# Output projection of a retention block by seven products of halves, with the work around it moved, on one Trainium2 core

## The chip, the cores and the metric

The kernel runs on one core of one Trainium2 chip. The metric is the device time of one execution in microseconds, lower is better. A core has five engines that run beside each other and wait for each other by semaphores: TensorE (PE in the profile; its weight loads are PEld), VectorE (DVE), ScalarE (ACT), GpSimd (POOL) and SyncE (SP), which here issues nearly all transfers.

## The reference

One attention-like layer and one feed-forward layer, each behind a layer norm and each inside a residual sum. x has 4 x 1024 tokens of 512 features.

```
# x: (4, 1024, 512)
h   = layernorm(x)
q   = h @ Wq.T                      # 512 x 512
v   = h @ Wv.T
ret = scan(v): state = lam * state + v_t    # along the tokens, lam by head
o   = layernorm(q * ret) * gamma + beta
o   = (o * silu(h @ Wg.T)) @ Wo.T
x   = x + layernorm(o)
h   = layernorm(x)
g   = silu((h @ fp8(gate_w)) * gate_scale)  # 512 -> 1536
u   = (h @ fp8(up_w)) * up_scale
x   = x + layernorm(((g * u) @ fp8(down_w)) * down_scale)
```

Here `fp8(w)` means that the weights are rounded to 8-bit values and used as float32 again.

## The kernel before

The 4096 tokens are cut into 8 blocks of 512 (`TB`), a block into 4 tiles of 128 tokens. A block t goes through `Retention` (the attention layer up to the normalised and turned x1) and then through `Ffn`. The main loop (L985 to L1205 or so) interleaves three of them: in its pass t it runs the feed-forward layer of block t (`f`), the retention of block t+1 (`b`), and the loading and normalising of x of block t+2 (`n`); `l` is the feed-forward layer of block t-1, whose last rows and final norm are finished in the first passes. Each pass t has 12 rows i (`NI`): in a row TensorE does the gate group (`f.gate(i)`, L1027), the up group (`f.up(i)`, L1088) and the down group two rows behind (`f.down(i - f.lag)`, L1155), eight matmuls each, and between them whatever the retention of the next block has due. "Block 1" in what follows means the pass t = 1 of this loop, "row" its i.

The order of the work on every engine is the order of the program text: `InOrder` (L66) wraps each engine, so that every instruction has line L74 in the profile and groups must be read by their tiles: `pfg`, `pfu`, `pd` are gate, up and down of the feed-forward layer, `pv`, `pq`, `pg` and `po` the four projections of the retention, `pt` a turn (transposition) by TensorE, `t_sums` the input sums, `mids` the partial results, `seen` the output of the search (below).

PSUM: the retention uses two banks, `pa0` and `pa1`, one buffer each; the gate and up groups use a ring of two (`pf`), into which the turns with home `"pf"` are taken as well; the down groups have four.

From block 2's retention on (`FAST`, so in passes t = 1 to 6) the v, q and g projections are not done as 16 full matmuls but in Strassen's manner by seven products of half size (`product`, L466). Each product is four matmuls of 128 x 256; its weight half (or a stored sum of halves) comes from a ring of four buffers `w_ring`, which `fetch_weights` (L369) refills over SP, one fetch behind each product. The right-hand sides are the halves of the turned x, or one of four differences `t_sums` that POOL makes (`input_sums`, L450). Products share two banks: some matmuls add onto a bank whose earlier content VectorE or ScalarE has to have read first. The order of the 21 products and their banks stand in `order` and `banks` (L332 to L336). The products are called at fixed places: behind the gate group (L1035), behind the up group (L1100), at the end of a row (L1169, L1176, L1180).

The output projection (`o`, L657) is direct in every block: rows 7 to 10 each do one tile of 128 tokens by four matmuls of 128 x 512 in full float32 from the weights in `wo_sb`. Behind each tile stand, on the tile's own result in PSUM: moments (`o_moments`, L665, VectorE and POOL), centring (`x1_of`, L668; `center_scale` on VectorE in these blocks), the residual addition (POOL) and its store (`kept`), moments of the sum (`x1_moments`), its normalising (`x1n_of`, VectorE), and the turn: tiles 0 to 2 by a VectorE transposition in small squares and a way through memory (`move_x1n` and `turn_by_blocks`, L311: four stores, one load), the last one by TensorE (`turn_x1n`). Both halves of the turned tile, the rounded upper and the remainder (`upper_of` on ScalarE, `rest_of` on VectorE), go into `x1nT`, which the next block's first gate group reads.

The x of the block after next is normalised on ScalarE (`norm_x`), transposed in squares on VectorE, stored (`send_x`) in rows 6 to 9, and fetched back turned (`fetch_x`) at the end of row 9. From block 3's x on, `norm_x` uses one buffer of tag `xn`, so each tile waits for the store of the one before.

In pass t = 1 ScalarE also searches all weights for values out of range in 24 steps (`find_over`, L223); the list `look` (L983) says how many of them each row takes, half of them behind the gate group and the rest later in the row (L1032, L1126).

Of the kernel before, what the change touches and what calls it, by code (L numbers as in the profile page):

```python
# [23 lines left out]
def retention_ffn_sandwich(  # L24
# [20 lines left out]
    NT, D = x.shape  # L45
# [177 lines left out]
    def find_over():  # L223


        k = 0
        for j in range(4):
            for w in (gate_sb, up_sb, down_sb):
                v = w[:, ts(j, NI // 4), :] if w is down_sb else w[:, :, ts(j, I // 4)]
                for sign in (1.0, -1.0):  # L230
                    tag = "ret" if k >= 16 else "xn"
                    seen = work.tile(list(v.shape), F8, tag=tag, name=f"seen_{k}", bufs=2 if k >= 16 else 1)
                    act.activation(
                        seen, v.bitcast(F32), AF.Relu, bias=neg_max, scale=sign,
                        accum_out=over[:, k : k + 1], saturate=False,
                    )
                    k += 1
                    yield
# [72 lines left out]
    def turn_by_blocks(dst, src, tag, name):  # L311


        t = work.tile([P, NQ, NC, Q], F32, tag=tag, name=name)
        dve.transpose(t, src.rearrange("p (c a i) -> p a c i", c=NC, a=NQ))
        m = dram.tile([P, NQ, NC, Q], F32, tag="turn", name=f"m{name}", bufs=2)
        for b in range(NQ):
            sp.dma_start(
                m[:, b].rearrange("(a i) c j -> i a (c j)", a=NQ),
                t[ts(b, Q)].rearrange("i a c j -> i a (c j)"),  # L320
            )
        sp.dma_start(dst, m)

# [12 lines left out]
    banks = {"v": {1: 0, 6: 1, 5: 0}, "q": {1: 1, 6: 0, 5: 1}, "g": {1: 0, 6: 0, 5: 1}}  # L336
    squares = {"v": (wvT, wv_sb), "q": (wqT, wq_sb)}
    operands = {}

# [16 lines left out]

    made = {}
    adding = weight_sums()

    def keep_sums(k):  # L360
        for j, t in made[k].items():
            operands[k][j] = dram.tile([P, 2, H], F32, tag=f"sum_{k}{j}", name=f"dsum_{k}{j}", bufs=1)
            sp.dma_start(operands[k][j], t)
# [5 lines left out]
    def fetch_weights():  # L369
        n = fetched[0]  # L370
        if n < total_products:
            k, j = order[n % len(order)]
            sp.dma_start(w_ring[:, n % RING], operands[k][j])
            fetched[0] += 1

    class Retention:
# [89 lines left out]
        def product(self):  # L466

            k, j = order[self.made]
            n = (self.t - FAST) * len(order) + self.made
            self.made += 1  # L470
            w = w_ring[:, n % RING]
            if j in (1, 6, 5):
                bank = ps_tile(f"p{k}{j}_{self.t}", f"pa{banks[k][j]}").rearrange("p (c f) -> p c f", c=2)
                if j == 6:
                    self.bank_b = bank
                else:
                    self.bank_a = bank
            bank = self.bank_b if j in (6, 7, 4) else self.bank_a
            for o in range(2):
                out_ = bank[:, o]  # L480
                if len(self.right[j].shape) == 4:
                    out_ = out_.rearrange("p (g j) -> p g j", j=Q)
                for c in range(2):
                    pe.matmul(
                        out_, w[:, c, ts(o, P)], self.right[j][:, c],
                        start=(j in (1, 6, 5) and o == 0 and c == 0), stop=True,
                        skip_group_check=True,
                    )
            fetch_weights()
            c12, p1, s167 = (mids[:, m] for m in (1, 2, 3))  # L490
            if j == 1:
                act.copy(p1, bank)
            elif j == 6:
                dve.tensor_tensor(c12, bank, p1, ALU.add)
            elif j == 7:
                dve.tensor_tensor(s167, bank, p1, ALU.add)
            elif j == 2:
                self.take(k, 0, 0, bank)
            elif j == 4:
                dve.tensor_tensor(p1, bank, p1, ALU.add)  # L500
                self.take(k, 1, 0, p1)
            elif j == 5:
                dve.tensor_tensor(s167, bank, s167, ALU.add)
                self.take(k, 1, 1, s167)
            else:
                dve.tensor_tensor(c12, bank, c12, ALU.add)
                self.take(k, 0, 1, c12)

        def take(self, k, o, h, src):

# [156 lines left out]

        def x1_of(self, s):  # L668
            self.x1n[s] = work.tile([P, D], F32, tag="tok", name=f"x1n_{self.t}_{s}", bufs=4)
            self.center(self.x1n[s], self.po.pop(s), self.mvo[s])  # L670
            pool.tensor_tensor(self.xt[s], self.xt[s], self.x1n[s], ALU.add)
            self.kept[s] = dram.tile([P, D], F32, tag="kept", name=f"kept_{self.t}_{s}")
            sp.dma_start(self.kept[s], self.xt[s])
# [18 lines left out]
        def move_x1n(self, s):  # L692

            x1n = self.x1n.pop(s)
            dst = x1n.rearrange("p (b c j) -> p b c j", b=NQ, c=NC)
            turn_by_blocks(dst, x1n, "ret", f"xs1_{self.t}_{s}")
            self.pt[s] = dst.rearrange("p b c j -> p c b j")

        def part(self, h, s):
            part = self.x1nT[:, h, :, ts(s, P)]  # L700
# [279 lines left out]

    look = [5, 5, 4, 2, 0, 0, 0, 2, 2, 2, 2, 0]  # L983
    l = None
    for t in range(NB):  # L985
        f, n = Ffn(a), None
        fast = b is not None and b.fast
        for i in range(NI):
# [28 lines left out]
                n.shift()  # L1017
            if b and not fast and i == 5:
                b.z(0)
            if b and i >= 8:  # L1020
                b.x1_moments(i - 8)
            if t == 0 and 8 <= i < 11:
                for _ in range(4):
# [49 lines left out]
            if b and 7 <= i <= 10:  # L1073
                b.o(i - 7)
            if b and i == 8:
                b.new_x1nT()
            if b and i >= 8:
                b.x1n_of(i - 8)
            if b and 8 <= i < 11:
                b.move_x1n(i - 8)  # L1080
            if b and i >= 9:
                b.upper_of(i - 9)
            if b and 7 <= i <= 10:
# [44 lines left out]
            if l and not b and i in (4, 5):  # L1128
# [3 lines left out]
                    l.rstd()  # L1132
            if n and i == 6:
                n.new_xnT()
            if b and 7 <= i <= 10:
                b.x1_of(i - 7)
            if b and i >= 9:
# [7 lines left out]
            if n and i == (9 if t else 7):  # L1145
                n.fetch_x()
            if b and n and i == 11 and t:
                b.rest_of(3)
            if t == 0 and i in (8, 9):
                keep_sums("vq"[i - 8])  # L1150

# [4 lines left out]
            elif l and i < 2 and (b or i == 0):  # L1156
                l.down(NI - 2 + i if b else NI - 1)
            if b and not n and i == 11:
                b.turn_x1n(3)
# [107 lines left out]
```

## Time and profile before

| | |
|---|---|
| Median of 3 runs | 984.25 us (983.97 to 984.66) |
| The profiled execution | 983.95 us, span 982.1 us |
| TensorE clock granted | 0.998 of full |
| `po` matmuls | 256 records, 114.5 us |
| `pv`, `pq`, `pg` matmuls by halves (all six blocks) | 1008 records, 238.4 us |
| DMA | 110.07 MB, mean 112 GB/s, 36.5% of the 16 engines |
| VectorE, longest groups | `fuse` remainders 74.5 us, `gate` products 71.7 us |

A full float32 matmul leaves two records in the trace. The profile gives, for each group of instructions, its count, its total and mean duration and what its engine waited for before it. The mean duration of a matmul is longer than its spacing[...]. Costs of TensorE's groups are therefore read from start to start.

### The profile page before, as it was taken

To read this page: it belongs to the slowest core of one execution; us is meant where nothing else is said; L and a number is where in the kernel's file an instruction comes from. 1 tells how busy PE (TensorE), PEld (TensorE's weight loads), DVE (VectorE), ACT (ScalarE), POOL (GpSimd) and SP (SyncE) were. 2 spreads that over 40 slices of the span, in tenths; PEclk is the share of its full clock that TensorE was granted. 3 is DMA by queue.
4 is the path that set the end of the run, shared out by engine and by line. 5 is a ranking of instruction groups with operands and counts; after the bars stand their busy time and mean duration, and the time that the engine had idled before them with its cause. 6 is when DMAs were issued, how large, how long until landed. Compare 5 with 4: busy or idle time off the path is not lost.

```text
span 982.1 us, 11265 instructions
## 1 busy us (share of the span) xinstructions
PE 963.9 (98%) x3950; PEld 734.3 (75%) x3950; DVE 663.3 (68%) x1019; ACT 369.9 (38%) x556; POOL 266.7 (27%) x346
## 2 busy tenths in 40 slices
PE   9999999989999999999999999999999999999996
PEld 7456656678876888678876788768887788877885
DVE  5996979655667667675686666766667765756445
ACT  3546655467645125221432215321152211512223
POOL 1405121412324033240513305133141322322020
PEclk9999999999999999999999999999999999999999
DMA  9311413752416426253243623245241542213021
GB/s 300 119 65 65 130 63 94 228 161 75 151 53 156 128 82 225 80 143 120 86 129 93 176 77 116 87 131 151 83 150 59 135 140 76 75 37 113 1 86 43
DMA packets 90936, 110.07 MB, mean 112 GB/s; under 512 B 8064, under 2 KB 55424, under 8 KB 90880
## 3 DMA queue, kind: packets, MB, share of 16 engines
q1 hardware_dynamic: 90016, 108.70, 36.5%
q8 instruction: 31, 0.51, 0.2%
q10 hardware_dynamic: 864, 0.66, 0.2%
q14 instruction: 25, 0.20, 0.1%
HBM read 76.56 MB, written 32.77 MB: 111 GB/s over the span
## 4 chain that ended last, share of the span: by engine, by line
PE 84%; DVE 7%; ACT 4%; POOL 2%; DMA 1%; issue 1%; SPq 0%; DVEq 0%; POOLq 0%; ACTq 0%
PE pfu L74 15%; PE pfg L74 15%; PE pd L74 15%; PE pq L74 10%; PE pv L74 10%; PE po L74 9%; PE pg L74 9%; DVE scr L74 1%; DVE st L74 1%; DVE gate L74 1%; PE idle L74 1%; DVE xs L74 1%; DVE fuse L74 1%; DMA xnT<-mx 1%; POOL sqsum L74 1%
## 5 line engine op out<-in xcount | busy, mean ns | idle before, releaser
L74 PE MATMUL pfu<-x1nT,up_sb 128*128 128x512 f32 x768 | 211.5, 417 | 0.3 <-DVE gate L74 0.3
L74 PE MATMUL pfg<-x1nT,gate_sb 128*128 128x512 f32 x768 | 195.4, 396 | 1.4 <-ACT gate L74 1.4
L74 PE MATMUL pd<-down_sb,fuse 128*128 128x512 f32 x720 | 186.5, 400 | 0.0
L74 PEld LDWEIGHTS pfu<-x1nT,up_sb 128*128 128x128 f32 x768 | 144.4, 188 | 43.0 <-issue 13.4
L74 PEld LDWEIGHTS pfg<-x1nT,gate_sb 128*128 128x128 f32 x768 | 144.2, 188 | 31.7 <-ACT gate L74 1.8
L74 PEld LDWEIGHTS pd<-down_sb,fuse 128*128 128x128 f32 x720 | 134.9, 188 | 27.4
L74 ACT CAST fuse<-gate 128x512 fp32r<-128x512 f32 x90 | 55.7, 618 | 235.5 <-DVE gate L74 235.5
L74 ACT ACTIVATE gate<-pfg,gs_sb 128x512 f32<-128x512 f32 x96 | 65.7, 685 | 193.0 <-PE pfg L74 192.9
L74 DVE SCALAR_TENSOR_TENSOR gate<-pfu,us_sb,gate 128x512 f32<-128x512 f32 x96 | 71.7, 747 | 72.3 <-PE pfu L74 69.8
L74 PE MATMUL po<-wo_sb,y 128*128 128x512 f32 x256 | 114.5, 592 | 0.0
L74 POOL TENSOR_SCALAR mv<-mv 128x1 f32<-128x1 f32 (+1 forms) x82 | 19.9, 243 | 299.0 <-DVE mv L74 298.0
L74 PEld LDWEIGHTS po<-wo_sb,y 128*128 128x128 f32 x256 | 48.2, 189 | 50.3 <-issue 46.3
L74 DVE TENSOR_TENSOR fuse<-gate,fuse 128x512 fp32r<-128x512 f32 x90 | 74.5, 827 | 12.1 <-ACT fuse L74 12.1
L74 POOL TENSOR_TENSOR ysum<-y 128x256 f32<-128x256 f32 (+1 forms) x14 | 14.0, 1000 | 189.9 <-DVE y L74 189.9
L74 POOL TENSOR_TENSOR x<-x,x1n 128x512 f32<-128x512 f32 x32 | 46.8, 1463 | 45.6 <-DVE x1n L74 36.7
L74 DVE BATCH_NORM_STATS2 st<-x 128x6 f32<-128x512 f32 x64 | 43.6, 681 | 13.7 <-POOL x L74 11.3
L74 POOL TENSOR_TENSOR mv<-mv,nhalf 128x1 f32<-128x1 f32 (+1 forms) x75 | 46.3, 617 | 6.2
L74 PE MATMUL pg<-t_sums,w_ring 128*128 128x256 f32 x192 | 45.6, 380 | 0.6 <-ACT mids L74 0.6
L74 PE MATMUL pv<-t_sums,w_ring 128*128 128x256 f32 x192 | 45.4, 379 | 0.8 <-POOL t_sums L74 0.8
L74 PE MATMUL pq<-t_sums,w_ring 128*128 128x256 f32 x192 | 45.3, 379 | 0.0
L74 PEld LDWEIGHTS pg<-t_sums,w_ring 128*128 128x128 f32 x192 | 35.9, 189 | 7.3 <-ACT mids L74 2.0
L74 PEld LDWEIGHTS pv<-t_sums,w_ring 128*128 128x128 f32 x192 | 36.2, 189 | 6.6 <-POOL t_sums L74 1.0
(150 smaller groups left out, 1337.3 us busy)
## 6 DMA issues: line engine op xcount, KB each, us to landing
kept<-x SPq DMA_DIRECT2D x32, 256.0 KB, 2.1
x<-kept SPq DMA_DIRECT2D x32, 256.0 KB, 4.1
x<-in_x SPq DMA_DIRECT2D x28, 256.0 KB, 4.1
out<-d SPq DMA_DIRECT2D x27, 256.0 KB, 2.0
xnT<-mx SPq DMA_DIRECT2D x24, 256.0 KB, 4.9
w_ring<-dsum_v SPq DMA_DIRECT2D x24, 256.0 KB, 2.7
w_ring<-dsum_q SPq DMA_DIRECT2D x24, 256.0 KB, 2.6
w_ring<-dsum_g SPq DMA_DIRECT2D x24, 256.0 KB, 2.7
```

Of the source, the lines that this page charges most:

```text
L74: return lambda *args, **kwargs: tc.keep_in_program_order(op(*args, **kwargs))
```

## The change

The output projection of passes t = 1 to 6 is done by seven products of halves too. Tokens take the place of the outer dimension there: the left side is a half of y or one of four sums of halves (`y_sums`: two on VectorE, two on POOL, kept in `t_sums`), the right side comes from the ring. The weight sums for it are made on VectorE in place in `wo_sb` in pass t = 1, row 0, and stored (`output_sums`, `keep_sums`). `add_o` gathers the products in `mids`: two copies on ScalarE, five additions on VectorE. The seven stand in rows 7 (three), 8 (three) and 9 (one). Everything behind the projection follows another order: it reads its tile from `mids` in SBUF and no longer from PSUM; centring is `shift_scale` on ScalarE (three instructions); tiles are taken in pairs, 0 and 1 in rows 8 and 9, 2 and 3 in rows 9 and 10; two tiles are moved through memory and two are turned by TensorE in row 11, where before it was three and one. `turn_by_blocks` hands back its load, so that both tiles' stores are issued first.

x of the block after next goes out in rows 6 (tile 0), 7 (tiles 1 and 2) and 8 (tile 3), and is fetched in row 8; two of its four input sums move from row 11 to row 9. The search of pass t = 1 gets pairs of numbers instead of halves: fewer steps in row 3, none in rows 9 to 11, more in rows 5 to 8. Two more of its steps use the buffer `xn`.

```diff
-                    tag = "ret" if k >= 16 else "xn"
-                    seen = work.tile(list(v.shape), F8, tag=tag, name=f"seen_{k}", bufs=2 if k >= 16 else 1)
+                    tag = "ret" if k >= 18 else "xn"
+                    seen = work.tile(list(v.shape), F8, tag=tag, name=f"seen_{k}", bufs=2 if k >= 18 else 1)
...
-        sp.dma_start(dst, m)
+        return lambda: sp.dma_start(dst, m)
...
+    order += [("o", j) for j in (1, 2, 6, 5, 3, 7, 4)]
+    banks = {
+        "v": {1: 0, 6: 1, 5: 0}, "q": {1: 1, 6: 0, 5: 1},
+        "g": {1: 0, 6: 0, 5: 1}, "o": {1: 0, 6: 1, 5: 0},
+    }
...
+    def output_sums():
+
+        v = woT.rearrange("(c p) f -> p c f", p=P)
+        b11, b12, b21, b22 = (wo_sb[:, i : i + 2, o : o + H] for i in (0, 2) for o in (0, H))
+        operands["o"] = {1: v[:, 0:2, 0:H], 2: v[:, 2:4, 0:H], 3: v[:, 2:4, H:D]}
+        made["o"] = {5: b11, 7: b12, 6: b22, 4: b21}
+        dve.tensor_tensor(b11, b12, b11, ALU.subtract)
+        dve.tensor_tensor(b12, b22, b12, ALU.subtract)
+        dve.tensor_tensor(b22, b22, b11, ALU.subtract)
+        dve.tensor_tensor(b21, b21, b22, ALU.subtract)
...
+                    if k == "o":
+                        left, right = self.left[j][:, c, ts(o, P)], w[:, c, :]
+                    else:
+                        left, right = w[:, c, ts(o, P)], self.right[j][:, c]
...
+        def y_sums(self, *which):
+            y = self.y
+            a11, a12, a21, a22 = (y[:, c : c + 2, ts(h, H)] for h in range(2) for c in (0, 2))
+            s1, s2, s3, s4 = (t_sums[:, k] for k in range(4))
+            self.left = {1: a11, 2: a12, 3: s4, 4: a22, 5: s1, 6: s2, 7: s3}
+            ops = {
+                1: (dve, s1, a21, a22, ALU.add), 2: (dve, s2, s1, a11, ALU.subtract),
+                3: (pool, s3, a11, a21, ALU.subtract), 4: (pool, s4, a12, s2, ALU.subtract),
+            }
...
+        def add_o(self, j, bank):
+
+            by_tile = mids.rearrange("p (r s) h f -> p r s h f", r=2)
+            c11, c12, c21, c22 = (by_tile[:, r, :, h, :] for r in range(2) for h in range(2))
+            if j == 1:
+                act.copy(c21, bank)
+            elif j == 2:
+                act.copy(c11, bank)
+            elif j == 6:
+                dve.tensor_tensor(c12, bank, c21, ALU.add)
+            elif j == 5:
+                dve.tensor_tensor(c22, bank, c21, ALU.add)
+            elif j == 3:
+                dve.tensor_tensor(c12, bank, c12, ALU.add)
+            elif j == 7:
+                dve.tensor_tensor(c22, bank, c22, ALU.add)
+            else:
+                dve.tensor_tensor(c21, bank, c21, ALU.add)
...
-            self.center(self.x1n[s], self.po.pop(s), self.mvo[s])
+            center = shift_scale if self.fast else self.center
+            center(self.x1n[s], self.po.pop(s), self.mvo[s])
...
-    look = [5, 5, 4, 2, 0, 0, 0, 2, 2, 2, 2, 0]
+    look = [(2, 3), (2, 3), (2, 3), (1, 0), (0, 0), (0, 2), (0, 3), (0, 2), (0, 1)] + 3 * [(0, 0)]
...
-            for _ in range(look[i] // 2 if t == 1 else 0):
+            for _ in range(look[i][0] if t == 1 else 0):
...
-            if fast and i in (0, 1, 2, 3, 4, 5, 6):
+            if fast and i < 10:
                 b.product()
...
+            if fast and i == 7:
+                b.y_sums(3, 4)
+            if fast and i == 9:
+                b.x1_moments(0)
+                b.x1_moments(1)
+            if fast and i == 10:
+                b.x1_of(2)
+                b.x1_of(3)
             if n and i == 11:
-                n.input_sums(1, 2, 3, 4)
+                n.input_sums(*((3, 4) if fast else (1, 2, 3, 4)))
             units()
             f.up(i)
             f.fuse(i)
+            if fast and i == 9:
+                loads = []
+                for s in range(2):
+                    b.x1n_of(s)
+                    loads.append(b.move_x1n(s))
+                for load in loads:
+                    load()
+                if n:
+                    n.input_sums(1, 2)
+            if fast and i == 11:
+                for s in range(2):
+                    b.upper_of(s)
+                    b.rest_of(s)
...
             if n and i == 11:
                 n.product()
                 if t:
-                    b.turn_x1n(3, "pf")
-                    b.upper_of(3)
+                    b.turn_x1n(2, "pf")
+                    b.upper_of(2)
...
                 b.gate_y(0)
                 b.gate_y(1)
+                b.y_sums(1, 2)
+            if n and t > 0 and i == 8:
+                n.norm_x(3, True)
+                n.send_x(3)
+            if fast and i in (7, 8):
+                b.product()
+            if n and t > 0 and i == 8:
+                n.fetch_x()
+            if fast and i == 8:
+                b.o_moments(0)
+                b.o_moments(1)
+                b.x1_of(0)
+                b.x1_of(1)
+            if fast and i == 9:
+                b.o_moments(2)
+                b.o_moments(3)
+            if fast and i == 10:
+                b.x1_moments(2)
+                b.x1_moments(3)
+                b.x1n_of(2)
+                b.x1n_of(3)
...
-            for _ in range((look[i] + 1) // 2 if t == 1 else 0):
+            for _ in range(look[i][1] if t == 1 else 0):
                 next(search)
...
-            if n and t > 0 and 6 <= i <= 9:
-                n.norm_x(i - 6, True)
-                n.send_x(i - 6)
+            if n and t > 0 and i in (6, 7):
+                for s in ([0], [1, 2])[i - 6]:
+                    n.norm_x(s, True)
+                    n.send_x(s)
...
             if b and not n and i == 11:
+                b.turn_x1n(2)
+                b.upper_of(2)
+                b.rest_of(2)
                 b.turn_x1n(3)
...
-            if t == 0 and i == 11:
+            if n and i == 11:
                 b.turn_x1n(3, "pf")
                 b.upper_of(3)
                 b.rest_of(3)
-            if fast and i < 3:
+            if fast and (i < 3 or i in (7, 8)):
                 b.product()
...
+            if t == 1 and i == 0:
+                output_sums()
+                keep_sums("o")
```

More of the change, by code (lines that the diff above doesn't have):

```diff
@@ L315, in turn_by_blocks @@
         dve.transpose(t, src.rearrange("p (c a i) -> p a c i", c=NC, a=NQ))
-        m = dram.tile([P, NQ, NC, Q], F32, tag="turn", name=f"m{name}", bufs=2)
+        m = dram.tile([P, NQ, NC, Q], F32, tag="turn", name=f"m{name}", bufs=3)
         for b in range(NQ):
@@ L335, in retention_ffn_sandwich @@
     order += [("g", j) for j in (1, 2, 6, 7, 4, 5, 3)]
-    banks = {"v": {1: 0, 6: 1, 5: 0}, "q": {1: 1, 6: 0, 5: 1}, "g": {1: 0, 6: 0, 5: 1}}
+    order += [("o", j) for j in (1, 2, 6, 5, 3, 7, 4)]
[3 more added lines that the diff above has]
+    }
     squares = {"v": (wvT, wv_sb), "q": (wqT, wq_sb)}
@@ L480, in product @@
                 out_ = bank[:, o]
-                if len(self.right[j].shape) == 4:
+                if k != "o" and len(self.right[j].shape) == 4:
                     out_ = out_.rearrange("p (g j) -> p g j", j=Q)
                 for c in range(2):
+                    if k == "o":
+                        left, right = self.left[j][:, c, ts(o, P)], w[:, c, :]
+                    else:
+                        left, right = w[:, c, ts(o, P)], self.right[j][:, c]
                     pe.matmul(
-                        out_, w[:, c, ts(o, P)], self.right[j][:, c],
+                        out_, left, right,
                         start=(j in (1, 6, 5) and o == 0 and c == 0), stop=True,
@@ L489, in product @@
             fetch_weights()
+            if k == "o":
+                return self.add_o(j, bank)
             c12, p1, s167 = (mids[:, m] for m in (1, 2, 3))
@@ L507, in product @@
                 self.take(k, 0, 1, c12)
+        def y_sums(self, *which):
[7 more added lines that the diff above has]
+            }
+            for k in which:
+                engine, dst, x, y, op = ops[k]
+                engine.tensor_tensor(dst, x, y, op)
+        def add_o(self, j, bank):
[15 more added lines that the diff above has]
+                dve.tensor_tensor(c21, bank, c21, ALU.add)
+            if j in (3, 4):
+                for s in (0, 1) if j == 3 else (2, 3):
+                    self.po[s] = mids[:, s].rearrange("p h f -> p (h f)")
         def take(self, k, o, h, src):
@@ L695, in move_x1n @@
             dst = x1n.rearrange("p (b c j) -> p b c j", b=NQ, c=NC)
-            turn_by_blocks(dst, x1n, "ret", f"xs1_{self.t}_{s}")
             self.pt[s] = dst.rearrange("p b c j -> p c b j")
+            return turn_by_blocks(dst, x1n, "ret", f"xs1_{self.t}_{s}")
         def part(self, h, s):
@@ L1019, in retention_ffn_sandwich @@
                 b.z(0)
-            if b and i >= 8:
+            if b and not fast and i >= 8:
                 b.x1_moments(i - 8)
@@ L1072, in retention_ffn_sandwich @@
                 b.z(3)
-            if b and 7 <= i <= 10:
+            if b and not fast and 7 <= i <= 10:
                 b.o(i - 7)
@@ L1076, in retention_ffn_sandwich @@
                 b.new_x1nT()
-            if b and i >= 8:
+            if b and not fast and i >= 8:
                 b.x1n_of(i - 8)
-            if b and 8 <= i < 11:
-                b.move_x1n(i - 8)
-            if b and i >= 9:
+            if b and not fast and 8 <= i < 11:
+                b.move_x1n(i - 8)()
+            if b and not fast and i >= 9:
                 b.upper_of(i - 9)
-            if b and 7 <= i <= 10:
+            if b and not fast and 7 <= i <= 10:
                 b.o_moments(i - 7)
+            if fast and i == 7:
[6 more added lines that the diff above has]
+                b.x1_of(3)
             if n and i == 11:
-                n.input_sums(1, 2, 3, 4)
+                n.input_sums(*((3, 4) if fast else (1, 2, 3, 4)))
             units()
@@ L1134, in retention_ffn_sandwich @@
                 n.new_xnT()
-            if b and 7 <= i <= 10:
+            if b and not fast and 7 <= i <= 10:
                 b.x1_of(i - 7)
-            if b and i >= 9:
+            if b and not fast and i >= 9:
                 b.rest_of(i - 9)
-            if n and t > 0 and 6 <= i <= 9:
-                n.norm_x(i - 6, True)
-                n.send_x(i - 6)
+            if n and t > 0 and i in (6, 7):
+                for s in ([0], [1, 2])[i - 6]:
+                    n.norm_x(s, True)
+                    n.send_x(s)
             if t == 0 and i in (5, 6):
@@ L1144, in retention_ffn_sandwich @@
                 n.send_x(2 * i - 9)
-            if n and i == (9 if t else 7):
+            if n and t == 0 and i == 7:
                 n.fetch_x()
             if b and n and i == 11 and t:
-                b.rest_of(3)
+                b.rest_of(2)
             if t == 0 and i in (8, 9):
@@ L1158, in retention_ffn_sandwich @@
             if b and not n and i == 11:
+                b.turn_x1n(2)
+                b.upper_of(2)
+                b.rest_of(2)
                 b.turn_x1n(3)
```

## The prediction

> **What bounds the kernel now.** I read the busy line first, then the chain of waits over block 1 (246 to 300 us), then the timelines of TensorE, ScalarE, VectorE, POOL and SP around one block's end, because the change edits that part.
>
> ```profile
> PE 963.9 (98%) x3950; PEld 734.3 (75%) x3950; DVE 663.3 (68%) x1019; ACT 369.9 (38%) x556; POOL 266.7 (27%) x346
> ```
>
> TensorE is busy 98% of the span, and tables of 20 us show 20.00 of 20 busy from 260 us on, but for 0.09 us per block. So time saved on TensorE counts, and a wait of TensorE counts in full. The chain gives the price of each group of matmuls:
>
> ```profile
> 269.77 1.73 PE pg L74 x8
> 271.49 1.83 PE pfu L74 x8
> 273.32 1.81 PE pd L74 x8
> 275.13 1.81 PE pfg L74 x8
> 276.94 3.43 PE po L74 x8
> 280.38 1.86 PE pfu L74 x8
> ```
>
> An FFN group is 1.81 us, a product of halves 1.73, a direct output tile 3.43. A turn by TensorE, and the end of a block (start, duration, engine, and idle time before it in brackets):
>
> ```profile
> 549.71 1.89 PE L74 MATMUL pv<-xnT,w_ring 128*128 128x256 f32 x8
> 551.69 0.63 PE L74 MATMUL pt<-ident,x1n 128*128 128x128 f32 x4
> 552.08 2.09 PE L74 MATMUL pd<-down_sb,fuse 128*128 128x512 f32 x8
> 554.00 1.89 PE L74 MATMUL pv<-t_sums,w_ring 128*128 128x256 f32 x8
> ...
> 550.00 1.26 POOL L74 TENSOR_TENSOR t_sums<-xnT 128x512 f32<-128x512 f32 x1
> 550.07 1.47 DVE L74 TENSOR_SCALAR x1n<-x,mv 128x512 f32<-128x512 f32 x1 [0.95 <-POOL mv L74]
> 551.34 1.34 POOL L74 TENSOR_TENSOR t_sums<-xnT,t_sums 128x512 f32<-128x512 f32 x1
> ```
>
> Here x1n takes 1.47 us on VectorE beside a POOL sum, against 0.55 elsewhere in the same block. Then the search of block 1 on ScalarE, and one store of x:
>
> ```profile
> 206.10 1.56 ACT L74 ACTIVATE seen<-gate_sb,neg_max 128x1536 fp8e4<-128x1536 f32 x1
> 207.80 1.58 ACT L74 ACTIVATE seen<-gate_sb,neg_max 128x1536 fp8e4<-128x1536 f32 x1
> ...
> 275.90 0.63 ACT L74 CAST fuse<-gate 128x512 fp32r<-128x512 f32 x1 [1.35 <-DVE gate L74]
> 276.43 0.81 ACT L74 ACTIVATE xn<-x,mv 128x512 f32<-128x512 f32 x1
> 277.14 0.67 ACT L74 ACTIVATE gate<-pfg,gs_sb 128x512 f32<-128x512 f32 x1
> ...
> 252.96 1.99 PE L74 MATMUL pg<-t_sums,w_ring 128*128 128x256 f32 x8 [0.64 <-ACT mids L74]
> ...
> 539.34 0.38 SPq L74 DMA_DIRECT2D mx<-xn  x1
> 541.63 1.91 SPq L74 DMA_DIRECT2D xnT<-mx  x4
> ```
>
> One search step costs 1.70 us from start to start. TensorE waited 0.64 us for ScalarE in block 1. A store of x lands 2.29 us after its issue (the fetch that needs it starts then).
>
> [...] I therefore take matmul costs from start to start, and place every moved instruction behind all that precedes it on its engine. [...]
>
> **The change part by part.** Steps are called j1, j2, j6, j5, j3, j7, j4 in their new order. Six blocks of the loop (t = 1 to 6) change. Clock times in steps 1, 2 and 6 to 9 are those of pass t = 4 in the profile before, with TensorE's new order laid out from 510.52 on; those in steps 4 and 5 are of t = 1, less 0.64 for step 3.
>
> 1. TensorE arithmetic. From the gate of row 7 (510.52) to that of row 11 (546.08) are 35.56 us: twelve FFN groups of 1.815 and, as the rest, 13.78 for four output tiles. A product takes 1.54 to the next start and makes the next FFN group 0.205 longer (2.02 for 1.815), so 1.745; seven are 12.2. Saved 1.57 a block, 9.4 in six.
>
> 2. One more tile is turned by TensorE instead of by DMA. From the product at 549.71 to the one at 554.00 are 4.29 us; a product and an FFN group alone are 1.54 + 2.02 = 3.56; 0.73 is left, 0.09 of it idle. So a turn is 0.64, six are 3.8. The 0.09 in each block goes (x1n comes earlier), 0.5 in six. Arithmetic in all: -9.4 + 3.8 - 0.5 = -6.1 us.
>
> 3. Block 1, row 3: one search step (1.70 us) less in front of the silu that TensorE waited 0.64 us for: -0.6.
>
> 4. Block 1, rows 5 to 7: search steps now stand at the end of row 5 (two), row 6 (three) and row 7 (two). In row 6, three of 1.70 follow the cast of fuse (275.90 - 0.64 = 275.26), then x of tile 0 (0.72) and the silu of the gate (0.58): 275.26 + 0.52 + 5.10 + 0.72 + 0.58 = 282.2. Only then comes the copy of j1 out of its bank, until 282.8. j2 adds onto the same bank and is due on TensorE at 274.33 + 1.82 + 1.54 + 2.02 = 279.7. TensorE waits 3.1 us.
>
> 5. Row 7 of the same block: copy of j2 at 284.8, two search steps until 288.7, x of tile 1 until 289.4, its transposition on VectorE until 290.2, its store 2.3, so x of tile 2 (same single buffer from block 3's input on) at 292.5 and its transposition until 294.0. On VectorE the additions of j6 and j5 are queued behind that transposition; with the remainder of fuse between them they end at 295.9. j3 adds onto j5's bank and is due at 293.5: 2.4 us more. Rows 5 and 8 hold a search step or two as well, but their silus come 1 to 2 us late against banks needed 3 us later.
>
> 6. The same queue in blocks 2 to 5, without search steps. The silu and copies run when the bank is full; x of tile 1 is at 518.8, tile 2 at 522.75 after the store, the transposition until 524.3, the addition of j5 until 526.1. j3 is due at 526.6. Hidden, with 0.4 us to spare; without that cover it costs what the store is late. VectorE's two y sums (0.6 us each) and POOL's two (1.3 each) collide with each other and with the remainder of fuse, which puts the gate's product at 517.0 instead of 516.2; its bank is wanted at 524.6, so this is free.
>
> 7. j1 needs y of chunk 1 after 0.43 us, where a direct tile needed it after 0.76; VectorE ends it at 512.75, j1's second pair is due at 512.77 with its weights 0.2 earlier. Bounds 0 and 0.35; I take 0.2 a block, 1.2 in all.
>
> 8. The end of blocks 1 to 5. Moments and x1 go: j4's addition until 536.2, moments of tiles 0 and 1 until 537.9, their x1n and transpositions until 541.2 (one x1n blocked by the earlier POOL input sums), moments of tiles 2 and 3 until 543, centring on ScalarE until 545.6, POOL's additions until 547.0, moments until 547.9, x1n of tile 3 from 548.87. POOL's last two input sums start then, as at 550.00 above: x1n ends at 550.35, the remainder of fuse is blocked until 552.0, and the gate's product of row 11 ends at 552.7. The second turn takes that PSUM bank and is due at 552.4: 0.3 us. The next gate group, due at 556.65, needs all four tiles; VectorE has them at 556.65. Bounds 0[...] and 1.2 (each step 0.2 later); I take 0.3, 1.5 in five blocks.
>
> 9. Block 6 has no products of a next block between turns and gate. There POOL is free, but ScalarE has five casts (0.52 each) after the last product at 550.35, so the last tile is ready at 553.8; TensorE is due at 553.05: 0.8 us. Bounds 0 and 1.3.
>
> 10. Costed at nothing: four weight sums on VectorE (2.7 us) and their four stores in block 1, row 0, where VectorE is 60% busy (12.04 of 20 us) and the addition wanted next ends a microsecond early; 42 more fetches of 256 KB on SP, each issued four products ahead and landing in 2.7 us; the kept stores and x1n loads on SP, whose second load lands near 548.6 against 551.8 wanted; the centring on ScalarE, 38% busy, for tiles 0 to 2. If the ring were late, each product would wait.
>
> Sum against the profiled execution's own 983.95 us: -6.1 - 0.6 + 5.5 + 1.2 + 1.5 + 0.8 = +2.3, 986.2. The median of the runs (984.25) is 0.3 above that execution, so 986.5.
>
> **The rivals.**
> - Clean ends: blocks 1 to 5 lose nothing at j1 and at the turns, block 1 still pays 5.5. -6.1 - 0.6 + 5.5 + 0.8 = -0.4, 983.9. For it: margins in steps 7 and 8 are tenths. Against: the blocked x1n is seen in every block.
> - Not slower, one mechanism: ScalarE reaches j1's copy in block 1 by the time j2 is due, so that the 5.5 goes. It would need the three search steps to run 3.1 us earlier, in the idle 3.43 before the mids silu at row 6; their place in the program is behind the cast, which speaks against it. -3.2: 981.1. From a lead of 2.9 us on this decides the sign.
> - The store of x, not the search, becomes the limit everywhere: landing at 3.4 us (the median over all transfers of that tile, fetches included) instead of 2.3, less the 0.4 of cover, stalls j3 for 0.7 in each of blocks 2 to 5: 986.5 + 2.8 = 989.3, and near 991 if the ends also pay 0.4 more each than I took. Against: SP has nothing else to issue then, and the stores of x that show their landing took 2.29.
>
> **How the numbers follow.** Forecast 0.58, clean ends 0.21, not slower 0.08, late store 0.13. From 983.0 to 990.0 holds the first, nearly all of the second and the start of the last. A measurement tells 0.2% (2 us) from no change: faster is below 982.3, slower above 986.2. The forecast lies just above the limit and its unknowns go mostly up: 0.50 of it slower, 0.08 same; with the rest, slower 0.63, same 0.29, faster 0.08.
>
> **What would show it.** Right: in block 1 TensorE idle before the second po group of row 7, released by ScalarE, near 3 us, and again before the fifth, released by VectorE, near 2.4; po groups 1.73 apart when adjacent work lets them; idle tenths before the second pt of each block. Wrong: no idle in block 1 (then faster), or idle before po groups in blocks 2 to 5 (then the store or VectorE's queue is the cause), or waits of TensorE for w_ring.

## The result and the profile after

The changed kernel takes 993.89 us (median of 4 runs, 991.54 to 994.03); the kernel before, timed beside it, 984.11 (4 runs, 983.97 to 984.66). The ratio is 1.0093, 95% interval 1.0079 to 1.0108: slower by 9.8 us, where 2.3 were forecast. The execution whose trace was taken is the quickest of the four, 991.54 us, span 989.8.

First the busy line of the changed kernel's page:

```profile
PE 961.7 (97%) x4118; PEld 765.0 (77%) x4118; DVE 674.3 (68%) x1035; ACT 406.9 (41%) x640; POOL 283.9 (29%) x358
```

TensorE is busy 2.2 us less (961.7 against 963.9) in a span 7.7 us longer, so it waits about 9.9 us more, and a part of its busy time is stretched by half clock (below). Where the loss lies, by pass of the main loop (from the first gate matmul of a pass to that of the next, the last one to the end of the span, us). "Again" is a second trace of the changed kernel (experiment 10), "best" a version told of below (experiment 9):

| pass | before | after | again | best |
|---|---|---|---|---|
| 1 | 118.73 | 123.70 | 122.08 | 116.27 |
| 2 | 117.75 | 117.95 | 118.11 | 116.48 |
| 3 | 117.51 | 117.88 | 117.79 | 116.23 |
| 4 | 117.55 | 117.68 | 117.77 | 116.23 |
| 5 | 117.53 | 118.00 | 121.21 | 116.23 |
| 6 | 114.09 | 113.72 | 113.75 | 112.89 |
| 7 | 75.63 | 76.56 | 76.56 | 75.78 |
| sum | 778.79 | 785.49 | 787.27 | 770.11 |

Ahead of pass 1 stand 203.27 us before and 204.28 after. Most of this 1.0 us is spent before pass 0 starts (94.20 and 95.18), which the change does not reach; that start lay between 94.1 and 95.2 in all kernels of this study.

Block 1 (pass 1) first. The chain of waits of the changed kernel, in order of time (start, duration, what):

```profile
276.00 0.62 ACT fuse L74
276.63 1.62 ACT seen L74 x3
278.25 1.32 issue
279.56 1.75 ACT seen L74 x3
281.31 0.71 ACT xn L74
282.02 0.57 ACT gate L74
282.59 0.48 ACT mids L74
283.07 0.04 issue
283.11 3.65 PE po L74 x8
...
293.91 1.82 PE pfu L74 x8
295.74 1.76 issue
297.50 1.97 PE po L74 x8
```

The chain leaves TensorE, which it did not do in these rows before (the prediction shows it there from 269.77 to 280.38 us). It follows the three search steps (`seen`, two instructions a step), x of tile 0 (`xn`), the silu (`gate`) and the copy of j1 (`mids`) on ScalarE, and only then comes j2. This is the queue that step 4 of the prediction wrote down, instruction by instruction. The same stretch in the timeline of TensorE (start, duration, and in brackets the idle time before it and what ended that):

```profile
278.56 2.21 PE L74 MATMUL pfu<-x1nT,up_sb 128*128 128x512 f32 x8
283.11 3.65 PE L74 MATMUL po<-w_ring,y 128*128 128x256 f32 x8 [2.34 <-ACT mids L74]
286.20 2.43 PE L74 MATMUL pd<-down_sb,fuse 128*128 128x512 f32 x8
...
297.50 1.97 PE L74 MATMUL po<-w_ring,t_sums 128*128 128x256 f32 x8 [1.76 <-issue]
```

and, ahead of the second wait, in those of ScalarE and VectorE (the last line is the addition of j5):

```profile
294.06 0.82 ACT L74 ACTIVATE xn<-x,mv 128x512 f32<-128x512 f32 x1 [2.84 <-DMA mx<-xn]
294.91 0.72 DVE L74 STREAM_TRANSPOSE xn<-xn 128x512 f32<-128x512 f32 x1 [2.95 <-ACT xn L74]
296.71 0.68 DVE L74 TENSOR_TENSOR mids<-po,mids 128x512 f32<-128x512 f32 x1
```

j2 waits 2.34 us. j3 waits 1.76 us: x of tile 2 itself waited for the store of tile 1, and the additions that free j3's bank stand on VectorE behind the transposition of x. j2 then takes 3.09 us to the next start (283.11 to 286.20) instead of 1.54. A table of 10 us stretches shows why. The number behind the busy times of the five engines is the granted TensorE clock:

```profile
275.00:285.00 10.00, 7.66 (x31) 5.80 (x30) 6.58 (x9) 7.68 (x11) 3.57 (x4) 0.91 0.13 39
285.00:295.00 10.00, 10.00 (x43) 8.33 (x42) 0.80 (x2) 5.36 (x8) 0.00 (x0) 0.92 0.21 66
295.00:305.00 10.00, 8.24 (x38) 6.68 (x37) 7.27 (x13) 4.15 (x9) 2.65 (x5) 1.00 0.56 173
```

0.09 and 0.08 missing over 10 us each are 3.4 us at half clock, from the end of the idle time on. In the second trace of the same kernel a wait of 2.35 us in the same place is not followed by it, j2 takes 1.65 us and pass 1 is 1.6 us shorter. So the half clock costs about 1.7 us, half of its length.

Then the end of a block, pass 3, in the timelines of TensorE, VectorE and POOL. (The prediction's times from 510 to 557 us in the kernel before are of pass 3 as well, which it calls t = 4; its sums do not hang on that number.)

```profile
557.06 2.09 PE L74 MATMUL pd<-down_sb,fuse 128*128 128x512 f32 x8
559.99 0.66 PE L74 MATMUL pt<-ident,x1n 128*128 128x128 f32 x4 [0.83 <-DVE gate L74]
```

```profile
556.09 1.48 DVE L74 TENSOR_SCALAR x1n<-x,mv 128x512 f32<-128x512 f32 x1 [0.72 <-POOL mv L74]
557.50 1.78 DVE L74 TENSOR_TENSOR fuse<-gate,fuse 128x512 fp32r<-128x512 f32 x1
559.20 0.74 DVE L74 SCALAR_TENSOR_TENSOR gate<-pfu,us_sb,gate 128x512 f32<-128x512 f32 x1
```

```profile
556.02 1.27 POOL L74 TENSOR_TENSOR t_sums<-xnT 128x512 f32<-128x512 f32 x1
557.25 1.47 POOL L74 TENSOR_TENSOR t_sums<-xnT,t_sums 128x512 f32<-128x512 f32 x1
```

Start by start this is step 8's picture: x1n and the remainder of `fuse` take 1.48 and 1.78 us beside POOL's two sums (0.55 and 0.69 without them, experiment 7), the gate's product comes last and frees the bank that the second turn wants. But the turn was due at 559.0 (the down group at 557.06, and the 1.94 us that it takes to the next start where nothing waits, in experiment 2); it is 1.0 us late, not 0.3. In passes 1 to 5 the idle time there is 0.83, 1.19, 0.83, 1.16 and 1.49 us, in the kernel before 0.09 a block in all.

### The profile page after: what moved, and what is told of

Read it like the earlier page. It is cut to its first block, busy times and chain, and to the rows that moved or that the text cites. A ratio compares the mean times of both kernels' runs of the same rounds, so it can differ in the third digit from the quotient of the medians.

```text
span 989.8 us, 11808 instructions
## 1 busy us (share of the span) xinstructions
PE 961.7 (97%) x4118; PEld 765.0 (77%) x4118; DVE 674.3 (68%) x1035; ACT 406.9 (41%) x640; POOL 283.9 (29%) x358
## 4 chain that ended last, share of the span: by engine, by line
PE 76%; DVE 12%; ACT 4%; POOL 3%; issue 3%; DMA 1%; SPq 0%; DVEq 0%; ACTq 0%
PE pfg L74 13%; PE pfu L74 12%; PE pd L74 11%; PE pq L74 10%; PE pv L74 9%; PE po L74 9%; PE pg L74 9%; DVE st L74 2%; DVE fuse L74 2%; ACT x1n L74 1%; POOL mv L74 1%; DVE gate L74 1%; DVE scr L74 1%; DVE xs L74 1%; POOL x L74 1%
## 5 line engine op out<-in xcount | busy, mean ns | idle before, releaser
L74 PE MATMUL pfu<-x1nT,up_sb 128*128 128x512 f32 x768 | 205.2, 409 | 0.4 <-DVE gate L74 0.4
L74 PE MATMUL pfg<-x1nT,gate_sb 128*128 128x512 f32 x768 | 198.3, 400 | 2.6 <-ACT gate L74 1.4
L74 PE MATMUL pd<-down_sb,fuse 128*128 128x512 f32 x720 | 189.1, 404 | 0.0
L74 POOL TENSOR_SCALAR mv<-mv 128x1 f32<-128x1 f32 (+1 forms) x82 | 22.8, 278 | 270.5 <-DVE mv L74 267.5
L74 PE MATMUL po<-w_ring,t_sums 128*128 128x256 f32 x192 | 45.5, 379 | 2.0 <-issue 2.0
L74 POOL TENSOR_TENSOR x<-x,x1n 128x512 f32<-128x512 f32 x32 | 42.0, 1316 | 13.4 <-ACT x1n L74 12.7
L74 PEld LDWEIGHTS po<-w_ring,t_sums 128*128 128x128 f32 x192 | 36.1, 189 | 8.4 <-issue 3.0
L74 DVE STREAM_TRANSPOSE xn<-xn 128x512 f32<-128x512 f32 x20 | 14.2, 709 | 40.8 <-ACT xn L74 40.8
```

The lines of the kernel that those rows point to most:

```text
L74: return lambda *args, **kwargs: tc.keep_in_program_order(op(*args, **kwargs))
```

## The experiments

All times are medians, ratios are to the kernel before in the same session.

**1. The search away from rows 5 to 7.** Changed kernel, one edit:

```
-    look = [(2, 3), (2, 3), (2, 3), (1, 0), (0, 0), (0, 2), (0, 3), (0, 2), (0, 1)] + 3 * [(0, 0)]
+    look = [(2, 3), (2, 3), (2, 3), (1, 0), (0, 0), (0, 2), (0, 0), (0, 0), (0, 1), (2, 0), (0, 0), (3, 0)]
```

> The changed kernel with five of block 1's search steps taken from rows 6 and 7 to rows 9 and 11, nothing else. Theory (three steps on ScalarE stand ahead of the copy of the first product, two ahead of x of tiles 1 and 2, and the wait also brings a stretch of half TensorE clock): both idle stretches of TensorE in block 1 (2.3 and 1.8 us in the changed kernel) and the half clock near 285 us go; 985.5 to 988 us against 993.9. Rival (the products and the second turn themselves cost the time, in every block, and the clock is lower whatever the search does): 992 to 994.

989.02 us (986.38 to 989.53, 5 runs), 1.0038 [1.0024, 1.0051], a little over the theory's range. Both waits of block 1 and the half clock there are gone (pass 1 is 117.79), the waits before the turns stay. Its runs differ with the granted clock of the execution: 986.38 and 986.96 us at 0.998, 989.02 and 989.07 at 0.996, 989.53 at 0.994. The trace is of the quickest.

**2. The gate's product of row 11 ahead of x1n of tile 3.** Changed kernel, with two calls moved behind `f.fuse(11)`:

```
-            if t > 0 and (t > 1 or i):
+            if t > 0 and (t > 1 or i) and not (fast and i == 11):
...
             if fast and i == 11:
+                b.x1n_of(3)
+                f.rest(10)
                 for s in range(2):
...
-                b.x1n_of(3)
```

> The changed kernel with row 11's gate product on VectorE put ahead of x1n of tile 3 and of the remainder of row 10's fuse, search untouched. Theory (the second turn waits for its PSUM bank, which that gate product frees late, behind a VectorE instruction blocked by POOL's input sums): the waits of 0.8 to 1.5 us ahead of the second pt of blocks 1 to 5 go and the end of block 6 gets shorter; 986 to 988.5 us against 993.9. Rival (the turn waits for x1n of tile 3 or for TensorE's own work, not for the bank): no more than 1 us gained, 993 to 994.

982.89 us (980.81 to 985.55, 20 runs), 0.9985 [0.9978, 0.9992]: 11.0 us gained by the medians, more than was expected. TensorE around the two turns of pass 3:

```profile
553.45 0.60 PE L74 MATMUL pt<-ident,x1n 128*128 128x128 f32 x4
553.81 2.10 PE L74 MATMUL pd<-down_sb,fuse 128*128 128x512 f32 x8
555.75 0.60 PE L74 MATMUL pt<-ident,x1n 128*128 128x128 f32 x4
```

No wait. x1n (1.49 us) and the remainder (1.78) are as slow as in the changed kernel and now cost nothing, since only the product holds a bank. The waits of passes 6 and 7 went as well (112.88 and 75.75). Block 1 keeps its waits (2.35 and 0.81 us) and, in this trace, the half clock behind the first (j2 takes 2.66 us there and the down group behind it 3.35, against 1.99 and 2.20 in the second trace of the changed kernel). Summed by pass the loop is 777.06 us, 8.4 below the first trace of the changed kernel, which is of its quickest run.

**3. Both edits.**

> Both edits of the two runs before. Theory (two independent losses): the gains add, 978 to 981 us, below the kernel before. Rival (one of them only moves the wait to the next limit, such as the additions behind x of tile 2): 984 to 988.

976.82 us (976.67 to 977.52, 4 runs), 0.9925 [0.991, 0.9939]. This is below the theory's range, and below both kernels. It is about what the change is worth once next to nothing waits for the moved work (0.30 us in pass 3 and 0.88 in pass 5 are left).

**4. The kernel before, with the changed kernel's search.** Its `look` and the buffers that go with it, nothing else.

> The kernel before with only the new list of search steps. Theory (the search costs only because a product's bank waits for a ScalarE copy behind it, and the direct projection has no such copy): 983.5 to 985.5 us. Rival (the steps in rows 5 to 8 load ScalarE too much by themselves): 987 to 990.

989.44 us (988.43 to 990.83), 1.0055 [1.0038, 1.0071]. The theory's number missed and the rival's time was hit, but by a mechanism that neither had named in this place. TensorE at the end of pass 1, first in the kernel before, then here:

```profile
314.61 1.97 PE L74 MATMUL pv<-xnT,w_ring 128*128 128x256 f32 x8 [0.29 <-DMA xnT<-mx]
```

```profile
317.94 3.65 PE L74 MATMUL pv<-xnT,w_ring 128*128 128x256 f32 x8 [3.63 <-DMA xnT<-mx]
```

In the kernel before, x of the next block is normalised on the same ScalarE, a row or two later than in the changed one; behind the search it is stored too late, and its fetch makes the next block's first product wait 3.63 us; that product then takes 3.65 us instead of 1.97, as long as j2 at half clock in the changed kernel. So the new search order costs the old kernel about 5 us too, by another way.

**5 to 7. One wait at a time, and POOL's sums.** On the version with both edits, two steps of the search in row 6 and none in row 7; then three in row 6 and none in row 7:

```
-    look = [(2, 3), (2, 3), (2, 3), (1, 0), (0, 0), (0, 2), (0, 0), (0, 0), (0, 1), (2, 0), (0, 0), (3, 0)]
+    look = [(2, 3), (2, 3), (2, 3), (1, 0), (0, 0), (0, 2), (0, 2), (0, 0), (0, 1), (0, 0), (0, 0), (3, 0)]
```

```
-    look = [(2, 3), (2, 3), (2, 3), (1, 0), (0, 0), (0, 2), (0, 0), (0, 0), (0, 1), (2, 0), (0, 0), (3, 0)]
+    look = [(2, 3), (2, 3), (2, 3), (1, 0), (0, 0), (0, 2), (0, 3), (0, 0), (0, 1), (0, 0), (0, 0), (2, 0)]
```

> The version with both edits (gate product of row 11 first, search spread; 976.8 us), with one more of its search steps put into row 6 of block 1 behind the cast of fuse: two there instead of none, none in row 9 and none in row 7. In the changed kernel three steps there made the second output product wait 2.34 us for ScalarE's copy. Theory (each step in that place costs its own 1.56 us of lateness, one for one, beyond the slack of 2.2 us that three steps of 1.56 less 2.5 late leave): two steps are 0.9 to 1.0 us late, so one wait of 0.8 to 1.0 before the second po group of row 7 in block 1, and 977.5 to 978.5 us if TensorE keeps its clock, 979 to 979.8 if that idle time brings a stretch of half clock. Rival (the wait comes from x behind the search, not from the copy): no idle there with none in row 7, 976.5 to 977.2.

977.78 us (977.34 to 978.47), 0.9929 [0.9914, 0.9943]; j2 waits 0.81 us and takes 1.99, so no half clock follows. One step fewer, 1.56 us less wait: lateness is counted off step by step, as the theory has it.

> The version with both edits (976.8 us), with three search steps in row 6 of block 1 as in the changed kernel, but none in row 7. Theory: the second output product waits 2.3 to 2.5 us for ScalarE, the fifth (which waited for x behind the two steps of row 7) does not wait; a stretch of half TensorE clock follows the idle time and costs 1.7 more: 980.5 to 981.5 us. Rival (the half clock came from both waits together, or from something else): 2.4 us alone, 978.8 to 979.6, with the granted clock at 1.00 throughout block 1. Rival (the fifth product's wait has nothing to do with row 7): both waits as in the changed kernel, 982 to 983.5.

981.87 us (980.05 to 983.0, 7 runs), 0.9972 [0.996, 0.9983], a little above the theory's range with the half clock; the two quickest runs lie between that range and the first rival's. TensorE in its trace, taken at 980.08 us:

```profile
282.93 1.99 PE L74 MATMUL po<-w_ring,y 128*128 128x256 f32 x8 [2.37 <-ACT mids L74]
284.57 2.19 PE L74 MATMUL pd<-down_sb,fuse 128*128 128x512 f32 x8
...
293.71 1.89 PE L74 MATMUL po<-w_ring,t_sums 128*128 128x256 f32 x8
```

j2 waits as in the changed kernel; j3, in the third line, no longer does: its wait needs the steps of row 7. And the clock stays whole: j2 takes 1.99 us. Two of the seven runs took 980.05 and 980.08 us at a mean clock of 0.998, the five others 981.17 to 983.0 at 0.995 to 0.996. One more stretch of 3.4 us at half clock lowers the mean by 0.0017 (an estimate: half of 3.4 us in the span of 978.3), so with the same wait it seems to come in some executions and not in others; the slower five are 1.1 to 2.9 us longer and have no trace.

The third of these is experiment 1's kernel without POOL's sums 3 and 4 at the end of passes 1 to 5 (pass 6 has none); that part of the computation is left out.

```
-            if n and i == 11:
-                n.input_sums(*((3, 4) if fast else (1, 2, 3, 4)))
+            if n and i == 11 and not fast:
+                n.input_sums(1, 2, 3, 4)
```

> The version with the search away (989.0 us), without POOL's two input sums at the end of passes 1 to 6: the sums 3 and 4 of the next block's first product series are not computed there (that computation is left out; nothing stands in its place). Theory (POOL's sums block VectorE[...], which stretches x1n of tile 3 from 0.55 to 1.48 us and the remainder of fuse from 0.66 to 1.78 us, and this is what makes the second turn wait for the gate's product): x1n 0.5 to 0.6, remainder 0.6 to 0.75, the waits of 0.8 to 1.5 us before the second turn gone, 981 to 984.5 us. Rival (the chain moments, centring, x1 is late by itself and the blocking is a detail): the waits shrink by half or less, 987 to 989.5.

979.36 us (978.65 to 979.56), 0.9943 [0.9928, 0.9958], 9.7 below its base and below the theory's range. VectorE in pass 3:

```profile
546.82 0.55 DVE L74 TENSOR_SCALAR x1n<-x,mv 128x512 f32<-128x512 f32 x1 [0.72 <-POOL mv L74]
547.28 0.69 DVE L74 TENSOR_TENSOR fuse<-gate,fuse 128x512 fp32r<-128x512 f32 x1
547.89 0.74 DVE L74 SCALAR_TENSOR_TENSOR gate<-pfu,us_sb,gate 128x512 f32<-128x512 f32 x1
```

x1n takes 0.55 us instead of 1.48 and the remainder 0.69 instead of 1.78. x1n starts no earlier against the turn (2.91 us before it, 2.90 before the due time in the changed kernel), yet in passes 1 to 4 no turn waits. The chain in front of x1n is thus not enough for the waits: they need both the blocking by POOL, taken away here, and the place of the product behind the blocked instructions, which experiment 2 changed.

**8. More buffers for x.** Changed kernel, x of every block in the buffers that the first blocks use (four, and two for the transposed x):

```
-            if self.t < 3:
+            if True:
```

in `norm_x` and in `send_x`.

> The changed kernel with x of every later block in buffers of their own (four and two of them) instead of the one that x of tile 2 waits for until the store of tile 1 has landed. Theory (the wait of 1.76 us before the fifth product in block 1 and the 0.24 in pass 4 are the store of x plus the search steps): those two waits go or shrink below 0.5, the 2.3 us before the second product stays, with its half clock; 991 to 992.3 us. Rival (the search steps of row 7 alone set it, the store is hidden beside them): the wait before the fifth product stays above 1.2 us, 993 to 994.2. Second rival (two buffers shared with other tiles make x or x1n wait elsewhere): slower than 994.3.

991.43 us (989.62 to 991.69, 4 runs), 1.0063 [1.0048, 1.0078], inside the theory's range. The wait of j3 in block 1 and the 0.24 us (in pass 3) are gone, j2's 2.35 stays with its half clock (j2 takes 3.51 us). So j3's wait needed both the search steps of row 7 and the store that x of tile 2 waits for: experiment 6 removed it by the one, this by the other.

**9. Experiments 3 and 8 together** ("best" in the table of passes).

> The version with both edits (976.8 us) and with the x buffers of the run before in it. Theory (with the search spread, the store of x stands in nobody's way but for 0.3 us before the fifth output product of pass 3; the time is TensorE's own work): that 0.3 goes, 976.3 to 976.8 us. Rival (x still waits for its store, hidden, and moves other work): 975 to 976. Rival (x and x1n share buffers and wait for each other): above 977.5.

977.12 us (976.43 to 977.61), 0.9918 [0.9902, 0.9935], in none of the ranges: the 0.3 us is gone from the trace, but the time is the same as experiment 3's within the runs. Its loop of 770.11 us has no TensorE wait of 0.2 us from pass 1's row 0 on. In pass 5 that is luck and not the buffers: the last store of x took 2.46 us in this execution (next experiment), while experiment 8, with the same buffers and a store of 4.0 us, waits 0.88 and 2.01 us there.

**10. The changed kernel once more.**

> The changed kernel as it is, looked at once more, because three of its four times lie 2.3 to 2.5 us above the one whose trace was taken (991.54). Theory (a second stretch of half TensorE clock follows one of its waits, beside the one in block 1 after the second output product): the trace shows two stretches of about 3.4 us at half clock inside the loop where the time is near 993.9, one where it is near 991.5, and no wait that is longer by 2 us. Rival (the clock is the same and a wait is longer, or a transfer is late): one stretch or none, and a new wait of 2 us.

993.46 us (one run), mean clock 0.996. One stretch of half clock in the loop, not two, a wait of 2.01 us that was 1.49 in the first trace, and a late transfer: this is the rival's picture, with the stretch in another place. Pass 1 is without the half clock (j2 takes 1.99 us). Pass 5 is 121.21 us instead of 118.00, on TensorE:

```profile
791.45 0.63 PE L74 MATMUL pt<-ident,x1n 128*128 128x128 f32 x4 [0.90 <-DVE x1n L74]
791.84 2.07 PE L74 MATMUL pd<-down_sb,fuse 128*128 128x512 f32 x8
795.91 0.66 PE L74 MATMUL pt<-ident,x1n 128*128 128x128 f32 x4 [2.01 <-DVE gate L74]
796.41 3.22 PE L74 MATMUL pv<-t_sums,w_ring 128*128 128x256 f32 x8
```

Both turns wait, and the product behind takes 3.22 us at half clock (the mean granted clock of 795 to 805 us is 0.83). The timelines of SP and of POOL in the same pass show where it begins, with the DMA view of 769 to 775 us under them (a queue with its packets, MB and share of 16 engines; then an issue with the us until it landed):

```profile
770.28 0.32 SPq L74 DMA_DIRECT2D mx<-xn  x1
774.39 1.91 SPq L74 DMA_DIRECT2D xnT<-mx  x4
```

```profile
783.29 1.62 POOL L74 TENSOR_TENSOR t_sums<-xnT,t_sums 128x512 f32<-128x512 f32 x1
785.00 0.19 POOL L74 TENSOR_SCALAR mv<-mv 128x1 f32<-128x1 f32 x1
```

```profile
q8 instruction: 1, 0.02, 1.7%
mx<-xn SPq DMA_DIRECT2D x1, 256.0 KB, 4.1
```

The last store of x lands 4.1 us after its issue, so x comes back 2 us later, POOL's sums 1 and 2 with it, and the moments of tiles 2 and 3 (`mv`) stand behind them on POOL. Measured from issue to the fetch that needs it, that store takes 2.04 to 2.11 us in passes 1 to 4 of the changed kernel's first trace, and 2.07 in pass 4 of experiment 3. In pass 5 it took 2.45 us in that first trace, 2.46 in experiment 9, 4.05 in experiment 3 and 4.11 in this trace; in experiments 7 and 8 it landed 4.3 and 4.0 us after its issue. What pass 5 has and pass 4 has not in this trace is a packet on the queue that the view calls `instruction`, at that very time (1.7% of 16 engines over 6 us: 1.6 us on one engine; in the first trace of the changed kernel, where the store took 2.45, 1.5% over 4 us: 1.0). That it delays the store is an inference that was not tried, and its length does not decide: in experiment 3 a packet of 0.96 us (1.2% over 5 us) stands beside a store of 4.05. The cause of the late store stays open. What it costs depends on the code behind: 3.2 us in this trace with the half clock, 1.1 us in experiment 3 (pass 5 is 117.30 there).

## Why the prediction was wrong in size

The direction and the places were right, the size was not: 986.5 with 983.0 to 990.0, measured 993.89. By its own steps, on the traces:

- Steps 1 and 2 (-6.1 in six blocks): the arithmetic gains more. Without waits a pass is 1.28 to 1.32 us shorter in passes 3 to 5 and 1.20 in pass 6, about -7.7 in six, with step 7's loss already in it. The mis-sized term is the second turn: from the product ahead of the turns to the one behind them are 4.46 us with two (experiment 3, 545.80 to 550.26) and 4.20 with one, so it costs 0.26, not 0.64. The prediction had put all that surrounds a turn on the turn. It also passed over a wait of 0.29 us in block 1 (314.61, above), which the change removes.
- Step 3 (-0.6): -0.9 (rows 0 to 6 of block 1: 70.79 after 71.70).
- Steps 4 and 5 (5.5): the mechanism was right, shown by experiments 5, 6 and 8. A search step takes 1.56 us back to back, not 1.70: j2 is 2.5 us late instead of 3.1, j3 1.9 instead of 2.4, together 4.4. No step had the half clock behind such a wait, 1.7 us in the traced run.
- Step 6 (0): right but for 0.24 us in one block, gone in experiment 8. Step 7 (0.2 a block): about 0.13, since j1 takes 1.67 us to the next start in pass 3 instead of 1.54.
- **Step 8 is the one that failed most.** It took 0.3 us for each of five block ends, 1.5 in all, with 1.2 for one as the upper bound. Measured lateness of the second turn is 1.0, 1.36, 1.0, 1.32 and 1.65 us, 6.3 in all. The mechanism is that of the text, shown by experiments 2 and 7, and the blocked stretch has the length it was given (x1n's start to the end of the product: 3.85 us, 3.83 forecast). The start of x1n is late: 2.90 us before the turn is due in pass 3 instead of 3.53, because centring ends 0.3 us later and the last moments, small instructions to and fro between VectorE and POOL, take 0.3 more than laid out. In passes 2, 4 and 5 it starts 2.56, 2.58 and 2.27 us before, and the turn is later by just that much; why the chain is slower there was not followed up. The step had laid out some fifteen instructions over three engines without a margin and taken the result as the middle.
- Step 9 (0.8): passes 6 and 7 lose 0.83 and 0.78 us against the best version, 1.6 together, beyond the bound of 1.3. The casts that it named start when row 11's product ends (910.49 us), and that product stands behind x1n and the remainder here too: experiment 2, which moves it, removes these waits.
- Step 10 (nothing): right; no wait of TensorE for `w_ring` appears in passes 1 to 6.

On the traced pair, of the 5.3 us that were not forecast (7.6 against 2.3), the ends of blocks give 4.8, the half clock 1.7, the start of the program 1.0 and step 9 0.8; arithmetic, block 1 and the wait passed over give back some 4. These leave about 1 us, up to four tenths a pass, that is not assigned. The median lies another 2.4 us higher, as three of the four executions do. The second trace, at 993.46, shows pass 5's late store with a half clock behind it; where the other executions lost their time is not known, since they have no trace.

Of the rivals, the late store was the wrong place: it hardly stalls j3 in blocks 2 to 5 and reaches TensorE in pass 5 by POOL's queue. "Clean ends" is what experiment 2 makes of the kernel: forecast 983.9, measured 982.89. That they lie so close is partly luck: the arithmetic gained more than it took, and the half clock in block 1 was not in it.

## What to carry to other kernels

A saving on a TensorE that is busy for 98% of the span, as here, is kept only if every bank that it wants is freed in time: find the one instruction that frees the bank and put it ahead of what merely happens to stand before it in its queue (moving two calls was worth 11 us here by the medians, 8.4 by the passes of two traces). Where a laid-out chain over several engines has only tenths to spare, price it at its upper bound at least, and allow for a TensorE wait that costs more than its length: behind five of the eight waits of 2.01 to 3.63 us in the table below the next groups were slower, in the changed kernel by about 1.7 us.

## What the hardware showed unexpectedly

The same wait was followed by half clock in some traces and not in others. In the first trace of the changed kernel 3.41 us at a granted clock of 0.50 follow j2's wait (stretch, length, TensorE's busy time first, the clock behind POOL's):

```profile
283.29:286.70 3.41, 3.41 (x9) 2.66 (x10) 0.71 (x2) 0.62 (x1) 0.00 (x0) 0.50 0.53 154
```

In its second trace the clock is whole around j2 and lower behind the turns of pass 5, where the 0.17 missing over 10 us are again 3.4 us at half clock:

```profile
275.00:285.00 10.00, 7.65 (x35) 5.98 (x33) 6.75 (x9) 7.68 (x11) 3.68 (x4) 1.00 0.11 32
285.00:295.00 10.00, 9.22 (x42) 7.44 (x40) 2.29 (x4) 5.80 (x8) 0.00 (x0) 1.00 0.24 74
...
795.00:805.00 10.00, 9.09 (x37) 7.63 (x37) 6.01 (x10) 3.80 (x7) 0.00 (x0) 0.83 0.24 66
```

These are all waits of TensorE of 1.99 us or more from row 0 of pass 1 on, in the twelve traces, with the duration of what stands behind them (us). "Turn" is the second turn of pass 5, and the product behind it is given:

| trace | the wait is before | wait | then takes |
|---|---|---|---|
| experiment 4 | the first product, end of pass 1 | 3.63 | 3.65 |
| changed kernel | j2, block 1 | 2.34 | 3.65 |
| experiment 8 | j2, block 1 | 2.35 | 3.51 |
| experiment 2 | j2, block 1 | 2.35 | 2.66, the down group behind it 3.35 |
| changed kernel, second trace | turn | 2.01 | 3.22 |
| changed kernel, second trace | j2, block 1 | 2.35 | 1.99 |
| experiment 6 | j2, block 1 | 2.37 | 1.99 |
| experiment 8 | turn | 2.01 | 1.89 |
| experiment 1 | turn | 1.99 | 1.89 |

The length of the wait does not decide by itself: 2.34 and 2.35 us were followed by slower groups in three traces, 2.35 and 2.37 in two others were not, and 2.01 us were once and once not. What else decides was not shown; no run shifted a wait on purpose to try it. So the same wait in block 1 cost about 1.7 us more in one trace of the changed kernel and nothing more in the other.
